# Attention scores of two heads: from stacked 128-row products to pairs of 64-row products

## The chip, the cores and the metric

The kernel runs on one core of a Trainium2 chip. The metric is the device time of one execution in microseconds, the median of several runs; smaller is better.

## The reference

The input is a batch of 4 sequences of 512 tokens with 512 features. A layer of attention with 16 heads comes first. Keys and queries have 64 features a head, values and gates 128, and there are 64 memory slots a head, filled by `s`. Both parts of the attention are running sums over tokens:

```python
z = cumlogsumexp(s, axis=2)          # over tokens
g = exp(shifted z - z); p = exp(s - z)
# keys:   hk = hk * g_t + k_t (x) p_t ;  ok_t = q_t . hk     (64 slots)
# pv = softmax(ok)
# values: hv = hv * g_t + p_t (x) v_t ;  ov_t = pv_t . hv    (128 features)
o = o * rsqrt(mean(o*o) + eps) * g_norm_weight
o = o * (gate * sigmoid(gate))
x = layernorm(x + o @ Wo)
x = layernorm(x + mixture(x))        # 8 experts of low rank, softmax over experts
```

Since `p` and `g` come from one cumulative sum, the recurrence can be written as masked products of matrices: with e = exp(s), the sum over earlier tokens of (q . k) e, divided by the cumulative sum of e, and likewise for values with the softmax weights and e in the place of q and k.

## The kernel before, in words

Every matrix product is made in a rounded 32-bit format (`F32R`). To keep the accuracy of 32 bits, an operand is split into hi, the rounded value, and lo, the remainder, and a product of two such operands is the sum hi·lo + lo·hi + hi·hi: three products on TensorE (PE). The split takes a copy (mostly on ACT) and a subtraction (mostly on DVE, sometimes on POOL).

The work is cut into 32 units: 4 sequences times 8 pairs of heads. `project_keys` computes for one unit the projections s, k and q (twelve products of 512 columns each), the exponentials `et`, the reciprocal `rc` of the cumulative sum, and a state `s1` of the first half of the sequence. `project_values` computes two gates and the values. `attend_keys` makes the scores of keys and, later, the softmax, the state `s2` and the weights `w`. `attend_values` makes the scores of values and then the normalised output, and `combine` multiplies by Wo and adds to `y`. The `mixture` of a finished sequence is woven into the next sequence's units.

The order of these generators is written out by hand in the strings FIRST, MIX, PLAIN and LAST, one letter a step, for one iteration of the main loop: A is `attend_keys` of unit n+1, B `attend_values` of unit n, p `project_keys` of n+2, v `project_values` of n+1, w `combine` of n-1, m the mixture, and x and y the sums. The framework keeps an instruction in this order on its engine's queue unless its own planning draws a later one ahead. [...] Weight blocks come by DMAs on SP's queue, split once and kept in memory as `kept_*`.

Scores work on chunks of 256 tokens (c = 0, 1). For one head and one chunk, `scores` makes a 128 x 384 tile `pa`: a block of 256 columns and one of 128, the causal part of a 256 x 256 square. Keys have 64 rows a head, half of the array. So `kst` (L265 to L269) holds hi in one half of the 128 rows and lo in the other half, for each head; `qst` (L289 to L293) holds the query's hi in both halves; and `qlo` (L294, L295) holds lo in one half and zeros in the other. Two products of 128 rows then give all three terms. The same is done for values with `est`, `wst` and `wlo`, and for the states `s1` and `s2`. ACT and DVE then split `pa` into `at` (L387, L388) and POOL sets the part above the diagonal to zero (`causal`, L186).

`keys_and_values` (letters x and y, one head each) adds up the state term and the products of `at` with `ee` (keys, 64 columns wide) and with `vh`, `vl` (values). It issues products of keys and of values in alternation.

PSUM has eight banks: two each for the pools `ps_pj` (projections), `ps_a` (scores), `ps_t` (transposes and small things) and `ps_o` (sums and outputs).

Of the kernel before, what the change touches and what calls it, by code (L numbers as in the profile page):

```python
# [8 lines left out]
F32 = mybir.dt.float32  # L9
# [9 lines left out]
def tile_abc_attention_ffn(  # L19
# [24 lines left out]
    P = 128  # L44
# [10 lines left out]
    NRAW = 5  # L55
    TMP = 7
    FIRST = "AvwwBvmAmxmBvBymApmppBAppwwAvp"
    MIX = "AvmBvAxvBmvyBmAwBpmppppwApwwA"
    PLAIN = "AvpBvAxBpvpyBvAwwABppAwwp"
    LAST = "AvBvAxBvvymABBppppwwApAwwp"  # L60

# [12 lines left out]
    ps_a = ctx.enter_context(tc.tile_pool(name="ps_a", bufs=2, space=PSUM))  # L74
    ps_t = ctx.enter_context(tc.tile_pool(name="ps_t", bufs=2, space=PSUM))
# [25 lines left out]

    picks = cpool.tile([P, NKT * P], F32R, name="picks")
    alphas = cpool.tile([P, T], F32R, name="alphas")
    qlo = cpool.tile([P, 2, T], F32R, name="qlo")
    wlo = cpool.tile([P, 2, T], F32R, name="wlo")

    def prep_zeros():
        for t in (qlo, wlo):
            for h in range(2):
                POOL.memset(f(t[64 * (1 - h) : 64 * (2 - h), h, :]), 0.0)  # L110
# [65 lines left out]
    def transpose_split(src, tb, th, tl):  # L176
        pt = ps_t.tile([P, NKT, P], F32, tag="pt", name="pt_x")
        ts = slice(tb * P, (tb + 1) * P)
        for kt in range(NKT):
            PE.transpose(pt[:, kt, :], src[:, tb, kt * P : (kt + 1) * P], ident)  # L180
        ACT.copy(th[:, :, ts], pt)
        DVE.tensor_sub(tl[:, :, ts], pt, f(th[:, :, ts]))

    def causal(at):
        v = at[:, 0:7:2, :]
        POOL.affine_select(v, f(v), [[0, 4], [1, P]], ALU.is_ge, 0.0, base=0, channel_multiplier=-1)  # L186
# [12 lines left out]
    def prep_ffn():  # L199
# [5 lines left out]
        for n in range(2 * NKT):  # L205
# [9 lines left out]
            pt = ps_t.tile([P, 512], F32, tag="pt", name="pt_f")  # L215
# [15 lines left out]
    def project_keys(u, p, xh, xl):  # L231
# [42 lines left out]
        pt = ps_t.tile([P, 512], F32, tag="pt", name="pt_e")  # L274
# [7 lines left out]
        u["eh"], u["el"] = eh, el  # L282
# [16 lines left out]
        pt = ps_t.tile([P, 2, P], F32, tag="pt", name="pt_k")  # L299
# [8 lines left out]
        pt = ps_t.tile([P, 2, P], F32, tag="pt", name="pt_s1")  # L308
# [10 lines left out]
        ACT.copy(s1[0:64, 0, :], sf[0:64, :])  # L319
        ACT.copy(s1[64:128, 1, :], sf[64:128, :])  # L320
        POOL.tensor_sub(s1[64:128, 0, :], sf[0:64, :], f(s1[0:64, 0, :]))
        POOL.tensor_sub(s1[0:64, 1, :], sf[64:128, :], f(s1[64:128, 1, :]))
# [3 lines left out]
    def project_values(u, p, xh, xl):  # L326
# [27 lines left out]
        u["vh"], u["vl"] = vh, vl  # L354
# [12 lines left out]
    def scores(kst, qst, qlo, h, c):  # L367

        pa = ps_a.tile([P, 512], F32, tag="pa", name="pa")[:, 0 : 3 * P]
        o = c * CH  # L370
        mm3(
            pa[:, 0:CH],
            [
                (kst[:, h, o : o + P], qst[:, h, o : o + CH]),
                (kst[:, h, o : o + P], qlo[:, h, o : o + CH]),
            ],
        )
        mm3(
            pa[:, CH : CH + P],
            [  # L380
                (kst[:, h, o + P : o + CH], qst[:, h, o + P : o + CH]),
                (kst[:, h, o + P : o + CH], qlo[:, h, o + P : o + CH]),
            ],
        )
        at = wk3.tile([P, 7, P], F32R, tag="at", name="at", bufs=4)
        pb = pa.rearrange("p (n t) -> p n t", t=P)
        ACT.copy(at[:, 0:3, :], pb)  # L387
        DVE.tensor_sub(at[:, 4:7, :], pb, f(at[:, 0:3, :]))  # L388
        causal(at)
        return at  # L390

    def accumulate(po, ops, stat, state, h, at, keys):

        kst, qst, qlo = ops
        state_terms = [
            (po[:, CH:T], state[:, h, :], qlo[:, h, CH:T], True, False),
            (po[:, CH:T], state[:, h, :], qst[:, h, CH:T], False, False),
        ]  # L400
        chunks = []
        for c in (1, 0):
            wide, narrow = state_terms if c else [], []
            o = c * CH
            a = at[c]
            sh, sl = stat(2 * c)
            for i, (l, r) in enumerate(((sl, a[:, 0:2, :]), (sh, a[:, 4:6, :]), (sh, a[:, 0:2, :]))):
                wide.append((po[:, o : o + CH], l, r, c == 0 and i == 0, i == 2 and keys))
            sh, sl = stat(2 * c + 1)
            for i, (l, r) in enumerate(((sl, a[:, 2, :]), (sh, a[:, 6, :]), (sh, a[:, 2, :]))):  # L410
                narrow.append((po[:, o + P : o + CH], l, r, False, i == 2 and not keys))
            chunks.append((wide, narrow))
        return chunks

    def issue(products):
        for o, l, r, start, stop in products:
            PE.matmul(o, l, r, start=start, stop=stop)  # L417

    def keys_and_values(h, ua, ub):


        hr = slice(64 * h, 64 * h + 64)
        ks = vs = [([], []), ([], [])]
        if ua:
            pk = ps_o.tile([P, 512], F32, tag="po", name="po_k")
            eh, el, rc = ua["eh"], ua["el"], ua["rc"]
            ks = accumulate(
                pk[0:64, :], ua["ops"], lambda n: (eh[:, n, hr], el[:, n, hr]), ua["s1"], h, ua["at"][h], True
            )
        if ub:  # L430
            pv = ps_o.tile([P, 512], F32, tag="po", name="po_v")
            hv = slice(h * DV, (h + 1) * DV)
            vh, vl = ub["vh"], ub["vl"]
            vs = accumulate(
                pv, ub["ops2"], lambda n: (vh[:, n, hv], vl[:, n, hv]), ub["s2"], h, ub["at2"][h], False
            )
        for (kw, kn), (vw, vn) in zip(ks, vs):
            issue(vw)
            for i in range(3):
                issue(vn[i : i + 1] + (kw[i : i + 1] if i < 2 else kn))  # L440
            issue(kw[2:])
        if ub:
# [6 lines left out]
            DVE.tensor_mul(t1, pv, ub["gate"][:, h, :])  # L449
# [4 lines left out]
            ub.setdefault("sq", []).append((t1, sqs))  # L454
        if ua:
            if h == 0:
                ua["okc"] = wk1.tile([P, T], F32, tag="tmp", bufs=TMP, name="okc")
            DVE.tensor_mul(ua["okc"][hr, :], pk[0:64, :], rc[hr, :])

    def both_scores(ops, h):  # L460
        at = {}
        for c in (1, 0):
            at[c] = scores(*ops, h, c)
        return at

    def attend_keys(u):
        rc = u["rc"]
        u["ops"] = u["kst"], u["qst"], qlo
        u["at"] = []
        for h in range(2):  # L470
            u["at"].append(both_scores(u["ops"], h))
            yield
        okc = u["okc"]
        pt = ps_t.tile([P, 512], F32, tag="pt", name="pt_ok")
# [19 lines left out]
        pt = ps_t.tile([P, 512], F32, tag="pt", name="pt_s2")  # L494
# [7 lines left out]
        ACT.copy(s2[64:128, 1, :], pt[64:128, DV : 2 * DV])  # L502
        DVE.tensor_sub(s2[64:128, 0, :], pt[0:64, 0:DV], f(s2[0:64, 0, :]))
        DVE.tensor_sub(s2[0:64, 1, :], pt[64:128, DV : 2 * DV], f(s2[64:128, 1, :]))
# [5 lines left out]
        pt = ps_t.tile([P, 512], F32, tag="pt", name="pt_w")  # L510
# [5 lines left out]
        ACT.copy(wst[0:64, 0, :], w[0:64, :])  # L516
        ACT.copy(wst[64:128, 1, :], w[64:128, :])
        DVE.tensor_copy(wst[64:128, 0, :], w[0:64, :])
        DVE.tensor_copy(wst[0:64, 1, :], w[64:128, :])
        DVE.tensor_sub(wlo[0:64, 0, :], w[0:64, :], f(wst[0:64, 0, :]))  # L520
        DVE.tensor_sub(wlo[64:128, 1, :], w[64:128, :], f(wst[64:128, 1, :]))

        u["w"] = wst, wlo
        yield

    def attend_values(u):
        u["ops2"] = u["est"], *u["w"]
        u["at2"] = []
        for h in range(2):
            u["at2"].append(both_scores(u["ops2"], h))  # L530
            yield
# [285 lines left out]
```

## Time and profile before

| | |
|---|---|
| median of 3 runs | 1491.17 us (1489.59 to 1491.31) |
| profiled execution, its own time | 1489.49 us |
| its span in the profile | 1487.7 us |
| granted clock of TensorE, mean | 0.997 |
| PE, weight loads, DVE, ACT, POOL busy | 94%, 81%, 78%, 59%, 38% |
| instructions | 23521, of them 8703 products |

The span is the time from the first to the last instruction of the program in the profile. In groups of instructions, the columns are the line and engine, the operation, the tiles (written <- read), the size, the count, then busy time in us and the mean duration in ns of one, and last the idle time of the engine ahead of them with what ended it. In the timeline the columns are start and duration in us. In the list of waits they are: who waited for whom, the total in us, the number of times, the longest.

### The profile page before, as it was taken

What the parts mean: (1) busy time and instruction counts of PE and PEld (TensorE: products, weight loads), DVE (VectorE), ACT (ScalarE), POOL (GpSimd) and SP (SyncE); (2) the same over time, 40 slices, a digit from 0 to 9 for tenths busy, and PEclk for the clock granted to TensorE, in tenths of its full rate; (3) what the DMA queues carried; (4) which work ended last, traced back from release to release, by engine and by line L of the source; (5) the groups of instructions that cost most, each with busy time, mean ns of one, the idle gap of its engine ahead of it and who ended that gap; (6) DMA issues with size and microseconds to landing.
All of it is one profiled execution on the core that took longest, in us unless ns stands there. A gap on an engine that the chain in (4) does not pass through costs nothing.

```text
span 1487.7 us, 23521 instructions
## 1 busy us (share of the span) xinstructions
PE 1403.8 (94%) x8703; PEld 1206.9 (81%) x8703; DVE 1159.1 (78%) x1888; ACT 879.9 (59%) x1731; POOL 560.0 (38%) x657
## 2 busy tenths in 40 slices
PE   7989999999999999999999999999999999999897
PEld 6778888878887888878888888888887778888675
DVE  3789888887888677887778678787878877767856
ACT  3676766666656555666666555456656565555432
POOL 6234434335434323333443343325433443343310
PEclk9999999999999999999999999999999999999999
DMA  6765555544333334443333333453333333333233
GB/s 195 251 214 203 185 174 187 189 151 142 123 118 135 128 123 146 156 157 115 115 126 113 129 128 128 136 191 113 116 125 115 128 128 105 109 128 114 107 134 128
DMA packets 94002, 212.32 MB, mean 143 GB/s; under 512 B 12992, under 2 KB 43712, under 8 KB 93888
## 3 DMA queue, kind: packets, MB, share of 16 engines
q1 hardware_dynamic: 93888, 210.82, 42.3%
q8 instruction: 69, 1.13, 0.3%
q14 instruction: 45, 0.37, 0.1%
HBM read 162.55 MB, written 48.23 MB: 142 GB/s over the span
## 4 chain that ended last, share of the span: by engine, by line
PE 43%; DVE 32%; ACT 9%; issue 7%; POOL 6%; DMA 2%; SPq 1%; DVEq 0%; POOLq 0%; ACTq 0%
PE ps_v L159 8%; PE ps_g L159 6%; PE po_y L159 5%; PE pa L159 4%; PE po_v L417 3%; PE po_k L417 3%; PE ps_vx L159 2%; DVE y L566 2%; PE po_f L159 2%; PE ps_h L159 2%; DVE cum L250 2%; POOL sqs L452 2%; DVE t L540 2%; DVE cum L245 2%; DVE at L388 1%
## 5 line engine op out<-in xcount | busy, mean ns | idle before, releaser
L186 POOL TENSOR_SCALAR_AFFINE_SELECT at<-at 128x512 fp32r<-128x512 f32 x256 | 171.5, 687 | 247.7 <-DVE at L388 232.7
L159 PE MATMUL po_y<-wt,oh 128*128 128x512 f32 x512 | 180.3, 404 | 5.5 <-DVE y L566 4.1
L388 DVE TENSOR_TENSOR at<-pa,at 128x384 fp32r<-128x384 f32 x256 | 133.5, 550 | 39.8 <-ACT at L387 38.3
L387 ACT CAST at<-pa 128x384 fp32r<-128x384 f32 x256 | 116.4, 479 | 57.7 <-PE po_v L417 37.5
L544 POOL TENSOR_TENSOR ol<-t,oh 128x512 fp32r<-128x512 f32 x64 | 88.8, 1401 | 151.0 <-ACT oh L543 140.0
L452 POOL TENSOR_SCALAR sqs<-sq 64x512 fp32r<-64x512 f32 x64 | 45.8, 716 | 210.7 <-DVE sq L451 203.5
L159 PEld LDWEIGHTS po_y<-wt,oh 128*128 128x128 f32 x512 | 96.2, 188 | 28.8 <-DVE y L566 8.1
L417 PE MATMUL po_v<-at,vh 128*128 128x256 f32 (+1 forms) x512 | 101.9, 252 | 0.0
L159 PE MATMUL po_y<-wt,ol 128*128 128x512 f32 x256 | 100.7, 394 | 0.9 <-POOL ol L544 0.9
L341 DVE SCALAR_TENSOR_TENSOR gate<-ps_g,gw_t,sg 128x512 f32<-128x512 f32 x64 | 47.8, 747 | 63.7 <-ACT sg L340 63.7
L566 DVE TENSOR_TENSOR y<-y,po_y 128x512 f32<-128x512 f32 x128 | 86.5, 682 | 12.8 <-PE po_y L159 11.4
L417 PE MATMUL po_k<-at,ee 128*64 128x128 f32 (+1 forms) x768 | 95.5, 251 | 0.0
L417 PEld LDWEIGHTS po_v<-at,vh 128*128 128x128 f32 x512 | 85.9, 189 | 0.0
L360 ACT CAST vh<-ps_v 128x512 fp32r<-128x512 f32 x64 | 37.4, 585 | 73.9 <-PE ps_v L159 73.9
L453 DVE TENSOR_TENSOR sqs<-sq,sqs 64x512 fp32r<-64x512 f32 x64 | 48.0, 750 | 31.7 <-POOL sqs L452 26.4
L159 PE MATMUL pa<-wst,est 128*128 128x128 f32 (+1 forms) x256 | 62.2, 275 | 10.7 <-DVE at L388 10.6
L417 PE MATMUL po_v<-at,vl 128*128 128x256 f32 (+1 forms) x256 | 65.5, 256 | 4.9 <-POOL at L186 4.8
L489 POOL TENSOR_TENSOR pr<-pr,rs 128x512 f32<-128x512 f32 x32 | 37.1, 1161 | 87.1 <-DVE rs L487 78.7
L449 DVE TENSOR_TENSOR t<-po_v,gate 128x512 f32<-128x512 f32 x64 | 44.3, 692 | 32.5 <-ACT sq L447 31.6
L417 PEld LDWEIGHTS po_k<-at,ee 128*64 128x64 f32 x768 | 68.8, 135 | 0.0
L361 DVE TENSOR_TENSOR vl<-ps_v,vh 128x512 fp32r<-128x512 f32 x64 | 44.0, 687 | 31.1 <-ACT vh L360 30.8
L159 PEld LDWEIGHTS pa<-wst,est 128*128 128x128 f32 x256 | 48.4, 189 | 18.2 <-DVE at L388 16.3
(330 smaller groups left out, 4317.6 us busy)
## 6 DMA issues: line engine op xcount, KB each, us to landing
wt<-kept_g SPq DMA_DIRECT2D x48, 512.0 KB, 3.4
wt<-kept_v SPq DMA_DIRECT2D x48, 512.0 KB, 3.3
wt<-kept_o SPq DMA_DIRECT2D x48, 512.0 KB, 3.4
wt<-kept_s SPq DMA_DIRECT2D x24, 512.0 KB, 3.9
wt<-kept_k SPq DMA_DIRECT2D x24, 512.0 KB, 3.6
wt<-kept_q SPq DMA_DIRECT2D x24, 512.0 KB, 3.3
kept_g<-wt SPq DMA_DIRECT2D x16, 512.0 KB, 3.0
kept_v<-wt SPq DMA_DIRECT2D x16, 512.0 KB, 3.3
```

The lines of the kernel that those rows point to most:

```text
L159: PE.matmul(out, l, r, start=first and i == 0, stop=last and i == n - 1)
L186: POOL.affine_select(v, f(v), [[0, 4], [1, P]], ALU.is_ge, 0.0, base=0, channel_multiplier=-1)
L341: DVE.scalar_tensor_tensor(gate[:, h, :], ps, gw_t, sg, ALU.mult, ALU.mult)
L361: DVE.tensor_sub(vl[:, 2 * t2 : 2 * t2 + 2, :], ps, f(vh[:, 2 * t2 : 2 * t2 + 2, :]))
L387: ACT.copy(at[:, 0:3, :], pb)
L388: DVE.tensor_sub(at[:, 4:7, :], pb, f(at[:, 0:3, :]))
L417: PE.matmul(o, l, r, start=start, stop=stop)
L449: DVE.tensor_mul(t1, pv, ub["gate"][:, h, :])
L452: POOL.tensor_scalar(sqs[0:64, :], sq, 1.0, 0.0, ALU.mult, ALU.add)
L453: DVE.tensor_sub(sqs[64:128, :], sq, f(sqs[0:64, :]))
L544: POOL.tensor_sub(ol, t1, f(oh))
L566: DVE.tensor_add(y[:, tb, :], y[:, tb, :], po)
```

## The change

The scores of the two heads are made as pairs of products over 64 rows. `kst`, `qst`, `est`, `wst`, `s1` and `s2` lose the stacking: heads lie on rows 0 to 63 and 64 to 127 as the projection leaves them, hi in one plane and lo in another. Each term is now three products (`thrice`), and `issue` takes one of head 0 and one of head 1 in turn. `attend` makes both chunks and the state terms of both heads in one run, into four `pa` banks and two `po` banks, and splits all four afterwards. `sum_keys` and `sum_values` are separate steps (letters x and y), each for both heads. `qlo`, `wlo` and their zeros go. The pool `ps_t` is merged into `ps_a`, which has four banks. `at` has six buffers of another layout for four, and the raw weights six for five. The order strings are new.

```diff
-    NRAW = 5
+    NRAW = 6
-    FIRST = "AvwwBvmAmxmBvBymApmppBAppwwAvp"
-    MIX = "AvmBvAxvBmvyBmAwBpmppppwApwwA"
-    PLAIN = "AvpBvAxBpvpyBvAwwABppAwwp"
-    LAST = "AvBvAxBvvymABBppppwwApAwwp"
+    FIRST = "BvvyAvmvxpmpABmwwBmpmpAwmAmpwp"
+    MIX = "BvvyAvvxpmpABmwwBmppAmwAmpwp"
+    PLAIN = "BvvyAvvxppABwwBppAwApwp"
+    LAST = "BvvyAvvxppABmwwBppAwApwp"
-    ps_a = ctx.enter_context(tc.tile_pool(name="ps_a", bufs=2, space=PSUM))
-    ps_t = ctx.enter_context(tc.tile_pool(name="ps_t", bufs=2, space=PSUM))
+    ps_a = ctx.enter_context(tc.tile_pool(name="ps_a", bufs=4, space=PSUM))
...
-        POOL.tensor_scalar(est[0:64, 0, :], et[0:64, :], 1.0, 0.0, ALU.mult, ALU.add)
-        POOL.tensor_scalar(est[64:128, 1, :], et[64:128, :], 1.0, 0.0, ALU.mult, ALU.add)
-        POOL.tensor_sub(est[64:128, 0, :], et[0:64, :], f(est[0:64, 0, :]))
-        POOL.tensor_sub(est[0:64, 1, :], et[64:128, :], f(est[64:128, 1, :]))
+        POOL.tensor_scalar(est[:, 0, :], et, 1.0, 0.0, ALU.mult, ALU.add)
+        POOL.tensor_sub(est[:, 1, :], et, f(est[:, 0, :]))
...
-        ACT.copy(kst[0:64, 0, :], ps[0:64, :])
-        ACT.copy(kst[64:128, 1, :], ps[64:128, :])
-        DVE.tensor_sub(kst[64:128, 0, :], ps[0:64, :], f(kst[0:64, 0, :]))
-        DVE.tensor_sub(kst[0:64, 1, :], ps[64:128, :], f(kst[64:128, 1, :]))
+        ACT.copy(kst[:, 0, :], ps)
+        DVE.tensor_sub(kst[:, 1, :], ps, f(kst[:, 0, :]))
...
-        ACT.copy(qst[0:64, 0, :], ps[0:64, :])
-        ACT.copy(qst[64:128, 1, :], ps[64:128, :])
-        ACT.copy(qst[64:128, 0, :], ps[0:64, :])
-        ACT.copy(qst[0:64, 1, :], ps[64:128, :])
-        DVE.tensor_sub(qlo[0:64, 0, :], ps[0:64, :], f(qst[0:64, 0, :]))
-        DVE.tensor_sub(qlo[64:128, 1, :], ps[64:128, :], f(qst[64:128, 1, :]))
+        ACT.copy(qst[:, 0, :], ps)
+        DVE.tensor_sub(qst[:, 1, :], ps, f(qst[:, 0, :]))
...
+    def thrice(out, stat, mov):
+        yield out, stat(1), mov(0)
+        yield out, stat(0), mov(1)
+        yield out, stat(0), mov(0)
+    def issue(groups, close=True):
+        groups = [list(g) for g in groups]
+        for i in range(max(map(len, groups))):
+            for g in groups:
+                if i < len(g):
+                    o, l, r = g[i]
+                    PE.matmul(o, l, r, start=i == 0, stop=close and i == len(g) - 1)
+    def attend(k, q, state, outs):
+        pas = {}
+        for c in (1, 0):
+            o = c * CH
+            groups = []
+            for h in range(2):
+                hr = rows_of(h)
+                pa = pas[c, h] = ps_a.tile([P, 512], F32, tag="pa", name="pa")
+                g = []
+                for a, n in ((0, CH), (P, P)):
+                    g += thrice(
+                        pa[:, P - a : P - a + n],
+                        lambda s: k[hr, s, o + a : o + a + P],
+                        lambda s: q[hr, s, o + a : o + a + n],
+                    )
+                groups.append(g)
+            issue(groups)
+        groups = []
+        for h in range(2):
+            hr = rows_of(h)
+            groups.append(list(thrice(outs[h][:, CH:T], lambda s: state[hr, s, :], lambda s: q[hr, s, CH:T])))
+        issue(groups, close=False)
+        ats = {}
+        for c in (1, 0):
+            for h in range(2):
+                at = ats[c, h] = wk3.tile([P, 3, 2, P], F32R, tag="at", name="at", bufs=6)
+                pb = pas[c, h][:, 0 : 3 * P].rearrange("p (n t) -> p n t", t=P)
+                ACT.copy(at[:, :, 0, :], pb)
+                DVE.tensor_sub(at[:, :, 1, :], pb, f(at[:, :, 0, :]))
+                causal(at)
+        return ats
...
+    def sum_keys(u):
+        ee, rc = u["ee"], u["rc"]
+        okc = u["okc"] = wk1.tile([P, T], F32, tag="tmp", bufs=TMP, name="okc")
+        for h in range(2):
+            pk, hr = u["pk"][h], rows_of(h)
+            accumulate(pk, lambda n, s: ee[:, n, s, hr], u["at"], h)
+            DVE.tensor_mul(okc[hr, :], pk, rc[hr, :])
+    def sum_values(u):
+        v = u["v"]
+        for h in range(2):
+            pv, hv = u["pv"][h], slice(h * DV, (h + 1) * DV)
+            accumulate(pv, lambda n, s: v[s][:, n, hv], u["at2"], h)
...
     def attend_values(u):
-        u["ops2"] = u["est"], *u["w"]
-        u["at2"] = []
-        for h in range(2):
-            u["at2"].append(both_scores(u["ops2"], h))
-            yield
+        u["pv"] = [ps_o.tile([P, 512], F32, tag="po", name="po_v") for _ in range(2)]
+        u["at2"] = attend(u["est"], u["w"], u["s2"], u["pv"])
+        yield
```

`wst`, `s1` and `s2` are changed as `qst` and `kst` are, and `attend_keys` as `attend_values`. In `accumulate`, each chunk is three wide and three narrow products of `at` as before, now on their own for keys and for values.

More of the change, by code (lines that the diff above doesn't have):

```diff
@@ L103, in tile_abc_attention_ffn @@
     alphas = cpool.tile([P, T], F32R, name="alphas")
[L104 to L108, printed above, removed]
-            for h in range(2):
-                POOL.memset(f(t[64 * (1 - h) : 64 * (2 - h), h, :]), 0.0)
     def prep_constants():
@@ L176, in transpose_split @@
     def transpose_split(src, tb, th, tl):
-        pt = ps_t.tile([P, NKT, P], F32, tag="pt", name="pt_x")
+        pt = ps_a.tile([P, NKT, P], F32, tag="pa", name="pt_x")
         ts = slice(tb * P, (tb + 1) * P)
@@ L184, in causal @@
     def causal(at):
-        v = at[:, 0:7:2, :]
+        v = at[:, 0:2].rearrange("p n s t -> p (n s) t")
         POOL.affine_select(v, f(v), [[0, 4], [1, P]], ALU.is_ge, 0.0, base=0, channel_multiplier=-1)
@@ L214, in prep_ffn @@
                 )
-            pt = ps_t.tile([P, 512], F32, tag="pt", name="pt_f")
+            pt = ps_a.tile([P, 512], F32, tag="pa", name="pt_f")
             for kt in range(NKT):
@@ L273, in project_keys @@
         yield
-        pt = ps_t.tile([P, 512], F32, tag="pt", name="pt_e")
+        pt = ps_a.tile([P, 512], F32, tag="pa", name="pt_e")
         for tb in range(NTB):
@@ L281, in project_keys @@
         DVE.tensor_sub(el, ptv, f(eh))
-        u["eh"], u["el"] = eh, el
+        u["ee"], u["eh"], u["el"] = ee, eh, el
         yield
@@ L289, in project_keys @@
         qst = wk2.tile([P, 2, T], F32R, tag="qst", name="qst", bufs=1)
-        ACT.copy(qst[0:64, 0, :], ps[0:64, :])
-        ACT.copy(qst[64:128, 1, :], ps[64:128, :])
-        ACT.copy(qst[64:128, 0, :], ps[0:64, :])
-        ACT.copy(qst[0:64, 1, :], ps[64:128, :])
-        DVE.tensor_sub(qlo[0:64, 0, :], ps[0:64, :], f(qst[0:64, 0, :]))
-        DVE.tensor_sub(qlo[64:128, 1, :], ps[64:128, :], f(qst[64:128, 1, :]))
+        ACT.copy(qst[:, 0, :], ps)
+        DVE.tensor_sub(qst[:, 1, :], ps, f(qst[:, 0, :]))
         u["qst"] = qst
         yield
-        pt = ps_t.tile([P, 2, P], F32, tag="pt", name="pt_k")
+        pt = ps_a.tile([P, 2, P], F32, tag="pa", name="pt_k")
         for tb in range(2):
@@ L305, in project_keys @@
         yield
-        pt = ps_t.tile([P, 2, P], F32, tag="pt", name="pt_s1")
+        pt = ps_a.tile([P, 2, P], F32, tag="pa", name="pt_s1")
         for tb in range(2):
@@ L318, in project_keys @@
         s1 = wk2.tile([P, 2, M], F32R, tag="s1", name="s1")
[L319 to L322, printed above, removed]
+        ACT.copy(s1[:, 0, :], sf)
+        POOL.tensor_sub(s1[:, 1, :], sf, f(s1[:, 0, :]))
         u["s1"] = s1
@@ L353, in project_values @@
         vl = wk2.tile([P, NTB, 2 * DV], F32R, tag="vl", name="vl")
-        u["vh"], u["vl"] = vh, vl
+        u["v"] = u["vh"], u["vl"] = vh, vl
         for t2 in range(2):
@@ L364, in project_values @@
         yield
[L367 to L401, printed above, removed]
+    def thrice(out, stat, mov):
[9 more added lines that the diff above has]
+                    PE.matmul(o, l, r, start=i == 0, stop=close and i == len(g) - 1)
@@ L402, in accumulate, with rows_of @@
+    def rows_of(h):
+        return slice(64 * h, 64 * h + 64)
+    def attend(k, q, state, outs):
+        pas = {}
         for c in (1, 0):
-            wide, narrow = state_terms if c else [], []
             o = c * CH
[L405 to L442, printed above, removed]
@@ new lines, in attend, with accumulate @@
+        return ats
+    def accumulate(out, stat, ats, h):
+        for c in (1, 0):
+            o = c * CH
+            at = ats[c, h]
+            terms = []
+            for a, n in ((0, CH), (P, P)):
+                terms += thrice(
+                    out[:, o + a : o + a + n],
+                    lambda s: stat(2 * c + a // P, s),
+                    lambda s: at[:, 1 - a // P : 1 - a // P + n // P, s, :],
+                )
+            for i, (o_, l, r) in enumerate(terms):
+                PE.matmul(o_, l, r, start=c == 0 and i == 0, stop=i == len(terms) - 1)
@@ L448, in keys_and_values @@
             t1 = wk1.tile([P, T], F32, tag="tmp", bufs=TMP, name="t1")
-            DVE.tensor_mul(t1, pv, ub["gate"][:, h, :])
+            DVE.tensor_mul(t1, pv, u["gate"][:, h, :])
             sqs = wk1.tile([P, T], F32R, tag="sqh", name="sqs", bufs=2)
@@ L453, in keys_and_values @@
             DVE.tensor_sub(sqs[64:128, :], sq, f(sqs[0:64, :]))
[L454 to L464, printed above, removed]
+            u.setdefault("sq", []).append((t1, sqs))
     def attend_keys(u):
         rc = u["rc"]
[L468 to L471, printed above, removed]
-            yield
+        u["pk"] = [ps_o.tile([P, 512], F32, tag="po", name="po_k")[0:64, :] for _ in range(2)]
+        u["at"] = attend(u["kst"], u["qst"], u["s1"], u["pk"])
+        yield
         okc = u["okc"]
-        pt = ps_t.tile([P, 512], F32, tag="pt", name="pt_ok")
+        pt = ps_a.tile([P, 512], F32, tag="pa", name="pt_ok")
         for tb in range(NTB):
@@ L493, in attend_keys @@
         vh, vl = u["vh"], u["vl"]
-        pt = ps_t.tile([P, 512], F32, tag="pt", name="pt_s2")
+        pt = ps_a.tile([P, 512], F32, tag="pa", name="pt_s2")
         terms = []
@@ L501, in attend_keys @@
         ACT.copy(s2[0:64, 0, :], pt[0:64, 0:DV])
-        ACT.copy(s2[64:128, 1, :], pt[64:128, DV : 2 * DV])
-        DVE.tensor_sub(s2[64:128, 0, :], pt[0:64, 0:DV], f(s2[0:64, 0, :]))
-        DVE.tensor_sub(s2[0:64, 1, :], pt[64:128, DV : 2 * DV], f(s2[64:128, 1, :]))
+        ACT.copy(s2[64:128, 0, :], pt[64:128, DV : 2 * DV])
+        DVE.tensor_sub(s2[0:64, 1, :], pt[0:64, 0:DV], f(s2[0:64, 0, :]))
+        DVE.tensor_sub(s2[64:128, 1, :], pt[64:128, DV : 2 * DV], f(s2[64:128, 0, :]))
         u["s2"] = s2
@@ L509, in attend_keys @@
         pnf = pn.rearrange("p n m -> p (n m)")
-        pt = ps_t.tile([P, 512], F32, tag="pt", name="pt_w")
+        pt = ps_a.tile([P, 512], F32, tag="pa", name="pt_w")
         for tb in range(NTB):
@@ L515, in attend_keys @@
         wst = wk1.tile([P, 2, T], F32R, tag="wst", name="wst")
[L516 to L523, printed above, removed]
+        ACT.copy(wst[:, 0, :], w)
+        DVE.tensor_sub(wst[:, 1, :], w, f(wst[:, 0, :]))
+        u["w"] = wst
         yield
     def attend_values(u):
-        u["ops2"] = u["est"], *u["w"]
-        u["at2"] = []
-        for h in range(2):
-            u["at2"].append(both_scores(u["ops2"], h))
-            yield
+        u["pv"] = [ps_o.tile([P, 512], F32, tag="po", name="po_v") for _ in range(2)]
+        u["at2"] = attend(u["est"], u["w"], u["s2"], u["pv"])
+        yield
         u["o"] = []
@@ L534, in attend_values @@
             t1, sqs = u["sq"][h]
-            pt = ps_t.tile([P, 512], F32, tag="pt", name="pt_ms")
+            pt = ps_a.tile([P, 512], F32, tag="pa", name="pt_ms")
             mm3(pt, [(meanw, sqs)])
@@ L607, in logits @@
         def logits(e, hh, hl):
-            lg = ps_t.tile([P, 512], F32, tag="pt", name="pt_lg")
+            lg = ps_a.tile([P, 512], F32, tag="pa", name="pt_lg")
             mm3(lg[0:40, :], [(w2c[:, e, :], hh), (w2c[:, e, :], hl)])
@@ L624, in weigh @@
         def weigh(kr, ps):
-            pt = ps_t.tile([P, 512], F32, tag="pt", name="pt_ab")
+            pt = ps_a.tile([P, 512], F32, tag="pa", name="pt_ab")
             mm3(pt, [(picks[:, kr * P : (kr + 1) * P], alphas)])
@@ L644, in mixture @@
         logits(NKT - 1, *hs)
-        pt = ps_t.tile([P, 512], F32, tag="pt", name="pt_al")
+        pt = ps_a.tile([P, 512], F32, tag="pa", name="pt_al")
         for tb in range(NTB):
@@ L665, in mixture @@
             pss[1] = low_rank(1)
-        pt = ps_t.tile([P, 512], F32, tag="pt", name="pt_alt")
+        pt = ps_a.tile([P, 512], F32, tag="pa", name="pt_alt")
         for tb in range(NTB):
@@ L733, in tile_abc_attention_ffn @@
         start(0)
-    prep_zeros()
     drain(gen(project_keys, 0))
@@ L756, in tile_abc_attention_ffn @@
         for c in plan:
-            if c in "xy":
-                keys_and_values("xy".index(c), ua, ub)
+            if c == "x":
+                if ua:
+                    sum_keys(ua)
+            elif c == "y":
+                if ub:
+                    sum_values(ub)
             else:
```

## The prediction

> **What bounds the kernel now.** I read the page first. TensorE (PE) is busy for 94% of the span, VectorE (DVE) for 78%, ScalarE (ACT) for 59%. The granted clock is full in all forty slices, so no time hides there.
>
> ```profile
> PE 1403.8 (94%) x8703; PEld 1206.9 (81%) x8703; DVE 1159.1 (78%) x1888; ACT 879.9 (59%) x1731; POOL 560.0 (38%) x657
> PEclk9999999999999999999999999999999999999999
> ```
>
> Busy PE is not PE at its peak, since a product's shown duration overlaps the next one's. So the second view is the timeline of PE alone, where the distance from start to start is what a product costs. This is one head's key scores, two groups of four, and the state terms and sums behind them:
>
> ```profile
> 715.83 0.28 PE L159 MATMUL pa<-qst,kst 128*128 128x256 f32 x1
> 715.95 0.28 PE L159 MATMUL pa<-qlo,kst 128*128 128x256 f32 x1
> 716.07 0.22 PE L159 MATMUL pa<-qst,kst 128*128 128x128 f32 x1
> 716.13 0.28 PE L159 MATMUL pa<-qlo,kst 128*128 128x128 f32 x1
> 716.25 0.33 PE L159 MATMUL pa<-qst,kst 128*128 128x256 f32 x1
> ...
> 716.71 0.33 PE L417 MATMUL po_v<-wlo,s 128*128 128x256 f32 x1
> 716.88 0.28 PE L417 MATMUL po_v<-wst,s 128*128 128x256 f32 x1
> 717.00 0.28 PE L417 MATMUL po_v<-at,vl 128*128 128x256 f32 x1
> ...
> 717.36 0.22 PE L417 MATMUL po_v<-at,vl 128*128 128x128 f32 x1
> 717.42 0.28 PE L417 MATMUL po_k<-qlo,s 128*64 128x256 f32 x1
> 717.54 0.22 PE L417 MATMUL po_v<-at,vh 128*128 128x128 f32 x1
> ```
>
> To be seen: a 256-column product costs 0.118 us and a 128-column one 0.06 us where they follow closely. At a change of group the last narrow one costs 0.12 and the first wide one 0.17, so a change costs about 0.11 us. And a 128\*64 product between 128\*128 ones costs no more than another. Third, what PE waits for, PEld being its weight loads:
>
> ```profile
> PEld pa L159 <- DVE at L388: 17.0, 28, 2.2
> PEld pt_k L301 <- ACT kf L272: 15.2, 12, 2.7
> PEld pt_w L512 <- issue: 10.9, 13, 1.9
> PE pa L159 <- DVE at L388: 10.6, 19, 1.8
> PE pt_w L512 <- DVE s L504: 6.6, 9, 1.4
> ```
>
> To be seen: named waits are short and many. The largest is the scores' own, for the two `pa` banks that DVE has not emptied. PE and PEld lines partly show one and the same wait, so I count the 17.0 and not the sum.
>
> **The change, part by part.**
>
> (1) *The products.* Before, a head's scores are 8 products (4 wide, 4 narrow) over all 128 rows, hi and lo stacked. One head takes 716.71 - 715.83 = 0.88 us, a pair of heads 1.76. State terms add 0.29 us a head for values (716.71 to 717.00) and 2 x 0.12 for keys, so 0.53 on average for two heads. A run of scores with its state terms costs 2.29 us. There are 2 x 32 = 64 runs: 146 us.
>
> After, each is three products over 64 rows, for two heads: 2 x (6 wide + 6 narrow + 3 wide of state terms) = 30 products instead of 20. At the trace's prices, one after the other: 18 x 0.118 + 12 x 0.06 = 2.84 us. If the two heads of a pair run at once on the two halves of the array: 1.42 us.
>
> No row of this trace shows a product over 64 rows. The two ends are these 1.42 and 2.84; the narrow pair has a bound of its own, because it still needs two weight loads, and loads are not seen closer than the narrow products, 0.06: between 0.06 and 0.12 a pair. The Trainium skill, "TensorE: Matmul & The Clock Gate", Part 3 (Packing small matmuls), says that products on different row groups run concurrently, starting about 4 ns apart, and gives 3.07 times for four 32-row tiles. That is 77% of the ideal; carried over to two tiles as an estimate it makes 2.84 / (2 x 0.77) = 1.85 us. With trace prices and the narrow pair in the middle (0.085) I get 9 x 0.118 + 6 x 0.085 = 1.57. I take 1.57, since the page's tiles differ in number and width; with 1.85 the sum is 18 us worse.
>
> (2) *Changes of group and mode.* Before, changes are inside the 2.29. After, a run has two inner changes (second chunk, state terms), 2 x 0.11 = 0.22, and enters and leaves the 64-row arrangement. On this the skill speaks against the change: "TensorEngine Tiling (Array Packing)", Key Properties, says that a change of tiling mode, unlike one of tile, drains TensorE. The trace's 128\*64 rows show no such price, but those use all rows, and no run here shows a change of rows. Low end: an ordinary group change, 0.11 us. High end: a wide product's whole shown duration exposed, 0.28. I take 0.16 (0.28 less the 0.118 that flows anyway), twice a run: 0.32. Without the rule it would be 0.22, and 6 us better in all.
>
> Run after: 1.57 + 0.22 + 0.32 = 2.11 us against 2.29: 0.18 x 64 = **11 us gained**.
>
> (3) *Wait for `pa`.* Two banks become four (the `ps_t` pool is merged into `ps_a`), and a run fills all four before anything needs emptying. The 17.0 us wait goes; I count **-15 us**. What is late next is in (6).
>
> (4) *The sums.* The 48 products a unit of keys and values stay, with the same forms. What goes is the alternation of keys and values, and narrow value products now follow each other with 128-column loads. In the scores such a narrow pair still costs 0.06 (716.07 to 716.13), so the bound is 0 to one group change for each of four accumulations a unit: 0 to 14 us; I take **+3 us**, as the alternation itself shows no gap removed.
>
> (5) *Conversions.* In natural layout one 128-row instruction does what two of 64 rows did, for the same time (ACT 591 ns at `ee` L280 for 128 rows, 580 at `qst` L290 for 64). For each unit: ACT loses one `kst`, three `qst`, one `wst`, one `s1` copy, 0.58 + 3 x 0.58 + 0.62 + 0.24 = 3.2 us; DVE loses one `kst` and one `qlo` subtraction, two `wst` copies (0.65 and 0.64 as means) and one `wlo` subtraction (0.81), 3.5 us; POOL's four `est` pieces (0.97, 0.92, 1.37, 1.58) become two, about -2.4 us, and one `s1` subtraction goes. Times 32: ACT -102, DVE -111, POOL -87. None bounds the span, so the worth is in PE's waits only. The chain `ps_k` to `kst` to `kf` to `pt_k` is shorter by one ACT and one DVE instruction (1.27 us), which covers most of the 15.2 us wait; the `w` chain is shorter by some 3 us of conversions. Together I take **-10 us** of the roughly 33 us in such rows above.
>
> (6) *New order and new waits.* Values' scores (B) now stand at the head of the iteration, straight behind the last steps of the one before. They need `w` split (DVE 0.69, ACT 0.62, DVE 0.69, about 2.2 us with hops), behind which lie only `pt_k`, one output block (1.4 us) and `pt_s1`: about 2.1 us of PE work. The fourth bank of a run is the one that `pt_s1` used, freed after two ACT and two DVE steps that answer each other (0.2 us each, but waits to 2.8 us). PE is in order, so all projections behind the run wait with it, and with them everything that ACT and DVE get from these. On POOL four `causal` selects (0.69 each) come together: `est`, `ol` and `sqs` queue up to 2.8 us behind them, and the sums wait for the last. Two projections, over 5 us, cover that. Bounds: 0 if the instruction order puts a projection in front, 0.5 us a run if not, 32 us; I take 0.16 a run, **+10 us**. If the cover of the `at` chain were gone, a run would pay 4 x 0.69 us.
>
> (7) *The rest.* The four memsets of `qlo` and `wlo` go (2 us on POOL at the start, off PE's path). NRAW 6 for 5 adds a load buffer: no DMA is added or removed on SP's queue, only the order of issues follows the new order string. First-batch units take 40.0 us with loads and 41 to 42 us in the last batch without, so loads do not bound: 0, at best -4.
>
> Sum: -11 - 15 + 3 - 10 + 10 = **-23 us**. The profiled execution took 1489.49 us (span 1487.7); minus 23 is 1466.5. The median shown is 1491.17, 1.7 above it: about **1467 us**, within 1445 to 1485 for this case alone. What can be told from no change is 0.2%, some 3 us.
>
> **The rivals.**
>
> *A: The pairs do not overlap.* Place: `attend`, 64 runs. Price: 2.84 + 0.54 = 3.38 us instead of 2.29, +70 us; with the other terms, -12: 1491 + 58 = about 1549. For it: no 64-row product is in the trace, and every product of one head and of the other still brings a weight load of its own. Against it: nothing in the trace, only the page. It decides from a run of 2.48 us (2.29 plus the 12 us of other gains over 64 runs), so from products of 1.94 us: pairs must realise 63% of their overlap (2.84 - 1.94 out of 1.42).
>
> *B: Pairs overlap, but the switches and the block form cost more.* Drain at 0.28 each and as much again for the refill, 128 times, +30 us, or the waits of (6) at their 32: 1467 + 30 = about 1500. For it: loads that cannot be drawn ahead across a switch. Against: a run has only two switches.
>
> *C: Everything goes well.* 1.42 us with changes at 0.11: 1.86 us a run, -28; -17 and -20 of waits, nothing for (4) and (6): about 1427.
>
> *D: Nothing.* The stream gains in (1) are used up by (2) and (6), and the shorter conversions were hidden anyway: 1491.
>
> **How the numbers follow.** Main case 0.36, C 0.12, D 0.07, A 0.27, B 0.18. Faster 0.48, same 0.07, slower 0.45: nearly even, because the one cost that decides is not in the trace. The range reaches from C to just short of A: 1430 to 1545, leaving out about 2 in 10.
>
> **What would show it.** Right: in the timeline the two heads' products of a pair start within some ns, the next pair 0.12 us later; a run about 2.1 us; no `pa` wait on `at`; DVE near 1050 us and ACT near 780 us busy. Wrong by A: starts of both heads 0.12 us apart, a run of over 3 us. Wrong by B: gaps of 0.3 us and more at the two ends of a run, or new waits of `pa` for `w` or for `sf`.

## The result, and the profile after

The changed kernel takes 1596.63 us (median of 4 runs, 1592.59 to 1599.72) against 1491.24 us: 7% slower, ratio 1.0705 (95% interval 1.0678 to 1.0733). The forecast of 1467 us, and its range up to 1545, were wrong. The first lines of the page already tell where to look:

```profile
span 1590.9 us, 24325 instructions
PE 1476.9 (93%) x9343; PEld 1271.3 (80%) x9343; DVE 1028.1 (65%) x1727; ACT 763.0 (48%) x1538; POOL 469.7 (30%) x559
PEclk9898998889999999899999998999999999999999
```

To be seen: DVE and ACT are relieved as forecast (1028 and 763 us; 1050 and 780 were named), and PE is busy for longer. The new thing is the clock row. It read nines throughout; now slices of 8 stand in it, and the mean granted clock is 0.947 instead of 0.997. The trace has only full and half clock, so a mean of 0.947 is 2 x 0.053 x 1590.9 = 169 us at half clock, against some 10 us before. Half of that is lost work: at most 84 us, against 5.

The list of what PE waits for names one new wait that is larger than all others together:

```profile
PE po_k L361 <- DVE t L435: 53.0, 31, 1.8
PE pa L361 <- DVE sf L299: 14.5, 15, 2.0
PE pa L361 <- DVE wst L491: 9.8, 21, 0.7
```

The wait occurs in 31 of 32 units, 1.7 us each. The timeline of one, PE first and then DVE, shows it:

```profile
694.77 1.60 PE L361 MATMUL pa<-qst,kst 64*128 64x256 f32 x24
696.21 0.28 PE L361 MATMUL po_k<-qst,s 64*64 64x256 f32 x1
698.22 0.56 PE L361 MATMUL po_k<-qst,s 64*64 64x256 f32 x5 [1.73 <-DVE t L435]
698.71 0.38 PE L149 MATMUL ps_v<-wt,x_1h 128*128 128x256 f32 x1
```

```profile
694.74 0.69 DVE L435 TENSOR_TENSOR t<-po_v,gate 128x512 f32<-128x512 f32 x1 [1.25 <-ACT sq L433]
695.35 0.67 DVE L437 TENSOR_TENSOR sq<-sq,sq 64x512 f32<-64x512 f32 x1
696.76 0.69 DVE L439 TENSOR_TENSOR sqs<-sq,sqs 64x512 fp32r<-64x512 f32 x1 [0.73 <-POOL sqs L438]
697.47 0.69 DVE L435 TENSOR_TENSOR t<-po_v,gate 128x512 f32<-128x512 f32 x1
```

To be seen: the 24 score products are quick, 1.44 us from 694.77 to 696.21. Then the state products of keys want the two `po` banks. The sums of values (y) ended just before the run, and their second head is still being read. That bank is free only after the second `t`, which ends at 698.16, since DVE first does `sqs` of head 0, which itself waits for POOL. The second state product starts at 698.22 where the first started at 696.21, and the projections stand in PE's queue behind it. Before, the state products were part of the sums, and no wait of PE for `t` was in the list.

What follows the stand is dearer than the stand. Four stretches of 3.4 us around it (the columns are the length, the busy us of PE, its weight loads, DVE, ACT and POOL, then the granted clock, DMA share and GB/s):

```profile
692.90:696.30 3.40, 3.40 (x43) 3.32 (x41) 1.87 (x3) 2.51 (x5) 0.19 (x1) 1.00 0.02 5
696.30:699.70 3.40, 1.67 (x16) 1.29 (x14) 2.90 (x5) 1.49 (x4) 1.28 (x3) 1.00 0.00 0
699.70:703.10 3.40, 3.40 (x18) 3.40 (x18) 2.48 (x3) 0.00 (x0) 2.15 (x4) 0.50 0.00 0
703.10:706.50 3.40, 3.40 (x21) 2.88 (x21) 0.69 (x1) 0.98 (x2) 0.00 (x0) 1.00 0.69 247
```

To be seen: PE was busy for 1.67 us of the second stretch. In the third it gets half the clock, although it has work all the time, and makes 18 products where 28 of 256 columns would fit at full clock. In the timeline, four products of 256 columns step by 0.48 us at full clock, ahead of the run, and by 0.85 us in the third stretch:

```profile
691.02 0.64 PE L149 MATMUL ps_v<-wt,x_1l 128*128 128x256 f32 x4
691.50 0.64 PE L149 MATMUL ps_v<-wt,x_1h 128*128 128x256 f32 x4
...
700.68 1.05 PE L149 MATMUL ps_v<-wt,x_1h 128*128 128x256 f32 x4
701.53 1.05 PE L149 MATMUL ps_v<-wt,x_1l 128*128 128x256 f32 x4
```

This trace has 39 stretches at half clock. Each lasts 3.41 us or a multiple of it, but for the last, which the end of the program cuts off. Of the 30 stands of 1.73 to 1.80 us at this place that the trace shows, 25 were followed by one.

The trace of the kernel before held the sign already, in its first unit. There PE stood for 2.23 us at the first `pt_k`, and the next stretch had half the clock:

```profile
26.60:30.00 3.40, 1.28 (x6) 0.70 (x4) 3.33 (x4) 1.43 (x3) 3.24 (x3) 1.00 0.00 0
30.00:33.40 3.40, 3.29 (x10) 2.81 (x11) 1.82 (x4) 2.17 (x5) 1.34 (x2) 0.50 0.37 135
```

The Trainium skill, "TensorE: Matmul & The Clock Gate", Part 1, describes such a gate: a free-running window of about 3.4 us in which activity is measured, and half the clock after a window of idleness; it warns of idle gaps over about 3.4 us. The length of the window agrees with the trace. The gap does not: by the page's figure none of these stands would have cost clock, and here one of 1.7 to 2 us is enough in most units.

### The profile page after: what moved, and what is told of

Same layout as the page of the kernel before. It is cut to its first block, busy times and chain, and to the rows that moved or that the text cites. A ratio compares the mean times of both kernels' runs of the same rounds, so it can differ in the third digit from the quotient of the medians.

```text
span 1590.9 us, 24325 instructions
## 1 busy us (share of the span) xinstructions
PE 1476.9 (93%) x9343; PEld 1271.3 (80%) x9343; DVE 1028.1 (65%) x1727; ACT 763.0 (48%) x1538; POOL 469.7 (30%) x559
## 4 chain that ended last, share of the span: by engine, by line
PE 74%; DVE 14%; ACT 6%; issue 2%; POOL 1%; DMA 1%; SPq 1%; ACTq 0%; DVEq 0%; POOLq 0%
PE ps_v L149 14%; PE ps_g L149 12%; PE po_y L149 9%; PE ps_s L149 5%; PE po_v L414 5%; PE ps_q L149 5%; PE po_k L414 4%; PE ps_k L149 4%; PE ps_h L149 3%; PE pa L361 3%; PE ps_vx L149 2%; DVE wst L491 2%; PE po_f L149 2%; DVE t L435 2%; DVE y L533 2%
## 5 line engine op out<-in xcount | busy, mean ns | idle before, releaser
L176 POOL TENSOR_SCALAR_AFFINE_SELECT at<-at 128x512 fp32r<-128x512 f32 x256 | 157.3, 643 | 74.1 <-DVE at L397 74.0
L244 POOL TENSOR_SCALAR est<-et 128x512 fp32r<-128x512 f32 x32 | 46.0, 1437 | 290.5 <-ACT et L233 290.4
L396 ACT CAST at<-pa 128x384 fp32r<-128x384 f32 x256 | 105.1, 491 | 9.8 <-PE pa L361 7.3
L318 ACT ACTIVATE sg<-ps_g 128x512 f32<-128x512 f32 x64 | 38.3, 599 | 135.1 <-PE ps_g L149 135.1
L361 PE MATMUL pa<-wst,est 64*128 64x256 f32 (+1 forms) x768 | 73.7, 303 | 26.7 <-DVE sf L299 14.2
L361 PEld LDWEIGHTS pa<-wst,est 64*128 64x128 f32 x768 | 60.0, 197 | 40.5 <-DVE wst L491 15.6
L141 DVE TENSOR_TENSOR wt<-wraw,wt 128x512 fp32r<-128x512 f32 x69 | 55.1, 801 | 57.6 <-ACT wt L140 56.9
L414 PE MATMUL po_v<-at,vh 128*128 128x256 f32 (+1 forms) x512 | 89.1, 281 | 0.0
L439 DVE TENSOR_TENSOR sqs<-sq,sqs 64x512 fp32r<-64x512 f32 x64 | 65.6, 1024 | 25.2 <-POOL sqs L438 24.2
L361 PE MATMUL po_k<-qst,s 64*64 64x256 f32 x192 | 29.7, 327 | 53.1 <-DVE t L435 53.0
```

Of the source, the lines that this page charges most:

```text
L141: DVE.tensor_sub(wt[:, 1, :], raw, f(wt[:, 0, :]))
L244: POOL.tensor_scalar(est[:, 0, :], et, 1.0, 0.0, ALU.mult, ALU.add)
L361: PE.matmul(o, l, r, start=i == 0, stop=close and i == len(g) - 1)
L396: ACT.copy(at[:, :, 0, :], pb)
L414: PE.matmul(o_, l, r, start=c == 0 and i == 0, stop=i == len(terms) - 1)
L439: DVE.tensor_sub(sqs[64:128, :], sq, f(sqs[0:64, :]))
```

## The experiments

Each time is a median; the kernel before ran on the same chip each time, at 1490.6 to 1491.0 us.

**State products out of the run (e1).** They are issued (by `states`) in front of the sums they belong to, still as pairs of both heads; `sum_values` is changed as `sum_keys` is.

```diff
-    def attend(k, q, state, outs):
+    def states(q, state, outs):
...
+    def attend(k, q):
...
     def sum_keys(u):
         ee, rc = u["ee"], u["rc"]
+        u["pk"] = [ps_o.tile([P, 512], F32, tag="po", name="po_k")[0:64, :] for _ in range(2)]
+        states(u["qst"], u["s1"], u["pk"])
...
```

> The state products leave the run of scores and stand in front of the sums of their own kind; both heads' pairs are kept. Theory 1 (wait, then clock): what costs is PE standing 1.7 us in each run of key scores for a po bank that VectorE has not yet read (53 us in all), and the half clock granted after such a stand (168 us at half clock, some 80 us of work lost). Then the wait for po is gone, time at half clock falls below 40 us, and the kernel takes 1470 to 1495 us. Theory 2 (64-row products themselves leave the array so little occupied that the clock is lowered, wait or no wait): the wait goes, -53, the mean clock stays near 0.95, about 1540 us.

Measured: 1495.5 us, ratio 1.003 (1.002 to 1.004), mean clock 0.985 (45 us at half). No wait of `po_k` for `t` is left. This one move takes back 101 of the 105 us. Theory 2 is out as the main cause: the 64-row products are all still there.

**The order alone (e2).** One projection comes between y and A, for instance `"BvvyAvvxpp..."` becomes `"BvvyvAvxpp..."`, in all four strings.

> Only the order strings are changed: one projection of values (24 products, 2.9 us) stands between the sums of values (y) and the run of key scores (A), and one less behind it. Theory 1: the po bank is free when the run comes to its state products, so the wait of 53 us goes and the clock with it: 1470 to 1500 us, less well than with late state products if the key sums now wait for at. Theory 2: clock near 0.95, about 1540 us.

Measured: 1508.26 us, ratio 1.0117 (1.0102 to 1.0132), clock 0.977. The wait for `po` is gone and 88 us are back, though it stays 8 us above the 1470 to 1500 expected; PE now waits 10.9 us in the key sums for POOL, with one projection as cover where there were two.

**The stand filled (e3).** Eight products that nothing reads stand between scores and state products in each run of key scores.

```diff
             issue(groups)
+        if fill is not None:
+            pf = ps_pj.tile([P, 512], F32, tag="pj", name="ps_fill")
+            mm3(pf, [(fill[:, 0:P], fill[:, 0:512])] * 8)
...
-        u["at"] = attend(u["kst"], u["qst"], u["s1"], u["pk"])
+        u["at"] = attend(u["kst"], u["qst"], u["s1"], u["pk"], u["ee"].rearrange("p a b c -> p (a b c)"))
```

> Adds work that nothing reads: eight 128-row products of 512 columns (1.8 us) between the score products and the state products of each run of key scores, so that the array works while it would stand. Theory 1: the stand is filled, the time lost in it (53 us) stays lost, but the clock is full, so about 1515 to 1530 us although 256 products are added. Theory 2: clock near 0.95 still, 1590 us or more. A third theory, that the clock falls by the change of row mode: two more switches a run, clock lower than 0.947, over 1600 us.

Measured: 1554.54 us, ratio 1.0438 (1.0417 to 1.046), clock 0.979. This parts the two costs. A filled run in its timeline:

```profile
634.16 1.60 PE L361 MATMUL pa<-qst,kst 64*128 64x256 f32 x24
635.69 2.09 PE L149 MATMUL ps_fill<-ee 128*128 128x512 f32 x8
637.71 0.56 PE L361 MATMUL po_k<-qst,s 64*64 64x256 f32 x6
```

The 2.02 us from 635.69 to 637.71 are lost as they were (696.21 to 698.22: 2.01 us). But with 256 products more the kernel is 42 us faster. That is the clock: time at half falls from 169 to 2 x 0.021 x 1558.8 = 65 us, and half of the difference is 52 us. It landed above the 1515 to 1530 expected, since a clock worth some 75 us had been assumed. The third theory, of changes between row modes, is out too: with two more of them a run the clock is higher.

**Pairs in another order (e5).** As e1, with all products of head 0 in front of those of head 1.

```diff
-        for i in range(max(map(len, groups))):
-            for g in groups:
-                if i < len(g):
-                    o, l, r = g[i]
-                    PE.matmul(o, l, r, start=i == 0, stop=close and i == len(g) - 1)
+        for g in groups:
+            for i, (o, l, r) in enumerate(g):
+                PE.matmul(o, l, r, start=i == 0, stop=close and i == len(g) - 1)
```

> As e1 (late state products), but all products of head 0 are issued before those of head 1, so no two heads' products stand side by side. If pairs overlap as the starts in the trace of the changed kernel suggest (24 products in 1.44 us), each run gets about 0.9 us longer with its state products: 40 to 60 us more than e1. If the overlap is worth nothing, within 5 us of e1. Theory 2 adds: half the array works for twice as long, so the clock falls further than in e1.

Measured: 1502.1 us, ratio 1.0092 (1.0059 to 1.0126): 7 us more than e1, not 40 to 60. The expectation failed because the edit does not part the heads in time. A run takes 1.88 us (607.08 to 608.96 in the timeline of PE), less than its products one by one (12 x 0.118 + 12 x 0.06 = 2.14), and starts of wide and narrow products mix in steps of 0.06 us. So some products of head 1 start ahead of earlier ones of head 0; whether the framework's own planning drew them ahead or the array took them out of turn, the trace does not tell. The written alternation is worth little, and the overlap had to be tested otherwise.

**Both heads on the same rows (e8).** As e1, but the score products of head 1 read head 0's rows (it leaves out head 1's scores).

```diff
-                hr = rows_of(h)
+                hr = rows_of(0)
                 pa = pas[c, h] = ps_a.tile([P, 512], F32, tag="pa", name="pa")
```

> As e1, but the score products of head 1 read head 0's rows, so that both heads' products use the same half of the array (leaves out head 1's scores; the number and size of products is e1's). If two products on different rows really run at once, a run of 24 takes 12 x 0.118 + 12 x 0.06 = 2.1 us or more instead of 1.53: +0.7 us in 64 runs, 1495 + 45 = about 1540, and the clock may fall, as half the array is busy for longer. If the starts 3 ns apart are only how the records are kept, it stays within 8 us of e1.

Measured: 1583.09 us, ratio 1.0619 (1.06 to 1.0639), 88 us over e1. A run of e1, then one of this kernel, each with the instruction behind it:

```profile
603.32 1.60 PE L361 MATMUL pa<-qst,kst 64*128 64x256 f32 x24
604.85 0.74 PE L149 MATMUL ps_v<-wt,x_1h 128*128 128x256 f32 x4
```

```profile
637.80 2.98 PE L361 MATMUL pa<-qst,kst 64*128 64x256 f32 x24
640.72 0.74 PE L149 MATMUL ps_v<-wt,x_1h 128*128 128x256 f32 x4
```

1.53 against 2.92 us: products on different rows do run at once. The 32 key runs make 32 x 1.39 = 44 of the 88 us. The value runs, which partly waited in e1, grow by 29 us in all (82 to 111 us, summed over the trace), and time at half clock rises from 45 to 2 x 0.03 x 1579.0 = 95 us, part of it in these same runs. So the 88 us are not the price of lost overlap alone. On the same rows narrow products cost as much as wide ones (2.92 / 24 = 0.12 us), which is more than the 2.1 us expected and has the cause that the next experiment shows.

**Sums apart in the kernel before (e9).** Values first, then keys, within each head.

```diff
-        for (kw, kn), (vw, vn) in zip(ks, vs):
-            issue(vw)
-            for i in range(3):
-                issue(vn[i : i + 1] + (kw[i : i + 1] if i < 2 else kn))
-            issue(kw[2:])
+        for vw, vn in vs:
+            issue(vw + vn)
+        for kw, kn in ks:
+            issue(kw[:2] + kn + kw[2:])
```

> The kernel before, with sums of values issued ahead of sums of keys instead of in alternation; all else as it was. The prediction's step 4 took 3 us for this, between 0 and 14. If alternation hides weight loads of the narrow value products: 1495 to 1505 us. If not: 1489 to 1494.

Measured: 1520.69 us, ratio 1.0199 (1.0182 to 1.0217): 30 us, beyond the bound of 14 that step (4) gave. One chunk of its values in the timeline:

```profile
703.09 0.23 PE L417 MATMUL po_v<-at,vl 128*128 128x128 f32 x1
703.15 0.38 PE L417 MATMUL po_v<-at,vh 128*128 128x128 f32 x2
703.37 0.33 PE L417 MATMUL po_v<-at,vl 128*128 128x256 f32 x1
```

And the weight loads there, on PEld:

```profile
703.09 0.30 PEld L417 LDWEIGHTS po_v<-at,vh 128*128 128x128 f32 x2
703.31 0.19 PEld L417 LDWEIGHTS po_v<-at,vl 128*128 128x128 f32 x1
```

To be seen: the first narrow product costs 0.06 us, the next two 0.22 together, and the loads of 128 columns also start 0.11 us apart. Behind a wide product of 0.118 us such a load is hidden; behind a narrow one of 0.06 it is not. In the same trace the narrow key products, whose loads have 64 columns, follow each other in 0.06 us. In the alternation of before, a wide key product stood between two narrow value products (717.36 to 717.54 in the prediction's lines), and none of them paid. One head's sums with their state terms take 2.91 us instead of 2.65 in most units of the two traces: 64 x 0.26 = 17 us, and PE's busy time rises by as much (1403.8 to 1421.4 us). Most of the rest are waits: with keys last, PE waits 12.2 us at the transposes of the key sums (`okc`), 0.8 before.

**Orders for the new layout (e6, e7, e10, e11, e12).** e6 is e1 with a gate projection ahead of the value scores and one for the next unit between key scores and their sums (PLAIN: `"vBvvyAvpxpABwwBppAwApwp"`).

> As e1 (late state products), with the order strings changed: a gate projection stands ahead of the run of value scores (B), and a projection for the next unit stands between the key scores and their sums. In e1 a run of value scores takes 2.42 us against 1.53 for keys, since it waits for w and for the bank of pt_s1 (14.7 and 4.4 us of named waits, and gaps at the chunk change). Theory 1 (what is left are waits of PE at the runs, and the half clock that follows some of them, 43 us in e1): value runs fall to about 1.55 us, -28 us, and half-clock time to some 20 us, -10: 1455 to 1475 us, faster than both kernels. Rival (the layout's gain is gone in switches of rows, and the waits are hidden elsewhere): within 8 us of e1, 1490 to 1500.

Measured: 1522.72 us, ratio 1.0214 (1.0199 to 1.023). The value runs got as short as expected (1.52 us), but the kernel is 27 us slower than e1, and a new wait took their place:

```profile
PE pt_ok L455 <- DVE okc L426: 48.3, 25, 3.3
```

Between x and the softmax step only one projection was left. Neither theory had this outcome.

e7 is the changed kernel with its state products in the run and PLAIN = `"vBvyvAvpxpABwwBppAwApwp"`, the others alike.

> The changed kernel with state products in the run, as handed over, and order strings that put a projection ahead of the value scores, one between these and their sums, one between the sums and the key scores, and two behind. Theory 1: the po wait goes as in e2 (1508) and the value runs get shorter as in e6: 1465 to 1490 us. If two switches of rows fewer a unit are worth what the timeline shows (0.2 us each at least), it can beat e6. Rival: sums of values now wait for at behind one projection only, and this eats the gain: over 1500.

Measured: 1493.41 us, ratio 1.0022 (1.0015 to 1.0029), clock 0.99, a little over the 1465 to 1490 expected: 41.6 us of the wait for `okc` again. The rival's wait for `at` is small (10.0 us).

e10 is e7 with two short steps that were due anyway ahead of the softmax step (PLAIN; the other three strings alike):

```diff
-    PLAIN = "vBvyvAvpxpABwwBppAwApwp"
+    PLAIN = "vBvyvAvpxpBwAwBppAwApwp"
```

> As e7 (state products in the run; projections ahead of the value scores and between the sums of values and the key scores), and the mean of squares and one output block (B, w) stand ahead of the softmax step, so that the key sums have 1.6 us more to reach VectorE's product before PE transposes it. In e7 PE waits 41.6 us for this. If that wait is all that separates e7 from the kernel before: 1493 - 35 = about 1455 to 1465 us, faster than both kernels. If it moves to the next step (softmax to the transposes of the weights): 1475 to 1490.

Measured: **1457.46 us**, ratio 0.9779 (0.9766 to 0.9793): as expected, 33 us faster than the kernel before and 139 us faster than the changed one, of which it differs in the four strings alone. The largest wait of PE is now:

```profile
PE po_v L414 <- POOL at L176: 7.8, 14, 1.3
```

e11 is e10 with late state products.

> As e10, but the state products stand in front of their sums, as in e1: two more changes between 64-row and 128-row products in each of 64 halves of units. By the timeline of the changed kernel, going in costs about 0.15 us at the last 128-row product and 0.10 at the first pair, going out 0.09 and 0.10, so about 0.4 us a visit: 64 x 0.4 = 26 us more than e10. If changes of rows are hidden: within 5 us of e10.

Measured: 1468.49 us, ratio 0.9844 (0.9831 to 0.9858), 11 us over e10. That is 0.17 us a place for two more changes of row mode in each of 64 half units, not 0.4. The lengths agree: 1.52 us for the scores and 0.52 for the state products where e10's run took 1.86. One run instead of two is worth something, but less than read off the timeline.

e12 is e10 with y and A adjoining again (`"vBvvyAv..."` for `"vBvyvAv..."`).

> As e10, with one letter put back: the sums of values (y) and the key scores (A) adjoin again, and the projection that stood between them stands ahead of y. Theory 1 (it is this adjacency that makes PE stand for the po bank and brings the clock down after it): a po wait of some 50 us returns, time at half clock rises from 37 to 120 us or more, and the kernel takes 1457 + 50 + 40 or more, 1545 to 1570 us. Rival (it was the order as a whole, or the value scores at the head of the iteration): within 20 us of e10.

Measured: 1547.26 us, ratio 1.0369 (1.0347 to 1.0391), 90 us more than e10, with clock 0.959 (2 x 0.041 x 1547.2 = 127 us at half) and the wait back:

```profile
PE po_k L361 <- DVE t L435: 53.7, 31, 2.5
```

Putting the neighbourhood in costs 90 us, taking it out gained 88 (e2): from both sides it is the cause of most of the 105 us.

## Why the prediction was wrong, point by point

*Step (6) failed.* It listed what the run at the head of an iteration waits for (`w`, the `pa` bank of `pt_s1`), and bounded new waits by 0 to 32 us. It left out the second resource that `attend` takes: both `po` banks, at the end of the run of key scores, 1.4 us after the sums that still occupy them. The two waits it named came, with 24 us together (the sign that rival B gave, though without its gaps of 0.3 us); the one it did not look at cost 53. The change moved the state products to where the last sums are still being read, and the prediction counted their products but not the buffers they write.

*The clock had no step.* The text read nines in all forty slices and concluded that no time hides there. But a slice is 37 us and 9 means 90% or more: the first one holds two stretches at half clock, 6.8 us, each behind a stand of PE of over 2 us. What a new stand does to the clock was not priced: 42 us measured in e3 (52 by the clock's own numbers). The wait and the clock together make 95 of the 105 us; e1, which takes away both, gives 101 back.

*Step (4) was mis-sized:* +3 us taken, bound 14. In the new layout the sums of a unit take 2.70 us for values and 2.11 for keys (626.05 to 628.75 in the timeline of e10, 705.91 to 708.02 in that of the changed kernel). Before it was 2 x 2.65 us less the 1.06 of state terms that step (1) counts, so 4.24: 0.57 us more in each of 32 units, 18 us. The cause is a misreading of an excerpt: "a change of group costs about 0.11 us" was in part the weight load behind the last narrow product (0.12 instead of 0.06), as e9 shows. The Trainium skill, "TensorE: Matmul & The Clock Gate", Part 2 (LDWEIGHTS), takes a load to last its columns divided by 1.2, in ns; by that an estimate for 128 columns is 107 ns. The 0.11 us of e9 agree; it was not weighed.

*Step (1) was right.* Pairs overlap, starts 3 to 4 ns apart, wide pairs 0.118 us, narrow ones 0.06 to 0.11 (0.085 was taken). Rival A is out (e8). The sum of rival B is loose: +30 us is what twice 0.28 - 0.16 makes in 128 switches; a drain of 0.28 and as much again, less the 0.16 already taken, would be 51.

*Step (2) was too dear.* A whole run of e10 with its state products takes 1.86 us (631.76 to 633.62 in its timeline), and the last wide product ahead of it 0.21 instead of 0.118: 1.95 us together, where 2.11 was forecast. The change of mode has a price, as the rule said, but by e11 a visit to the other row mode costs 0.17 us.

*Steps (3) and (5) held in what went away:* the wait of `pa` for `at` and most of that at `pt_k` are gone. DVE lost 131 us and ACT 117. What that is worth by itself no run shows.

*The sum of the mechanism,* 1467 us, is near what the layout gives under a fitting order (1457). That is partly luck: by the lengths above the runs gain 64 x (2.29 - 1.95) = 22 us and not 11, and the sums lose 18 and not 3, so two errors nearly cancel. The forecast costed the layout and took the order strings as a detail; these decided.

What stays open is what the gate measures. The count in the last section says what goes with half clock; no run tried a stand of a set length, so no threshold is given.

## What to carry to other kernels

When work is moved to an earlier place, list the buffers that it writes as well as those it reads, and ask who still reads the last contents: a bank is taken at the first product into it. Price a new stand of TensorE of 2 us with the clock that may follow, not only with its length; a row of nines before the change says nothing on that. And judge a layout only under an order made for it: the same code under two orders took 1597 and 1457 us.

## What the runs showed of the hardware

- A stand of 1.7 to 2 us next to 64-row products was followed by 3.4 us or more at half clock in most units (25 of 30; 169 us at half in all). 256 added products that filled the stand made the kernel 42 us faster.
- Both the idle time and the 64-row products go with half clock. The table cuts each of the thirteen traces into windows of 3.41 us, set by the times at which its clock changes, and takes those at full clock. It counts how many had half the clock in the next window. Windows with 1 to 7 of these products are left out. It is a count over kernels that are much alike, not an experiment.

| PE idle in the window | no 64-row product | 8 or more of them |
|---|---|---|
| under 0.7 us | 0 of 3708 | 16 of 757, 15 of these in e8 |
| 0.7 to 1.2 us | 0 of 148 | 35 of 73 |
| 1.2 to 1.8 us | 8 of 102 | 53 of 54 |
| over 1.8 us | 29 of 31 | 11 of 11 |

- Products on different halves of the rows overlap: 1.53 us for 24 products written in turn, 1.88 written head by head, 2.92 all on one half.
- A narrow product (128 columns) costs 0.11 us where the product ahead is narrow too and the loads have 128 columns; it costs 0.06 behind a wide product, or where the loads have 64 columns (e9).
- A further visit to the 64-row arrangement cost 0.17 us on average (11 us for 64, e11).
